# A two-layer perceiver: layer 0 stores each transposed memory in DRAM, layer 1 loads it and folds its layer norm into weights and one scale

## The chip, the core and the metric

The kernel runs on one core of one Trainium2 chip. The metric is the device time of one execution in microseconds. A core has TensorE (PE in the profile, with its weight loads listed apart as PEld), VectorE (DVE), ScalarE (ACT), GpSimd (POOL) and SyncE (SP, which here only issues DMAs). All data is float32.

## What is computed

The input is a query array x of 16 x 64 x 256 and a memory ctx of 16 x 1601 x 256. Six blocks are each added to x: cross attention over ctx with a top-32 softmax, retention and a transformer layer with a mixture of experts (layer 0); cross attention over ctx with 16 heads, random features and a tree of small networks (layer 1). Both cross attentions read the same memory. The one in layer 1 normalises it first:

```python
kn = layernorm(ctx, norm_w, norm_b)          # (ctx - mean) * rsqrt(var + 1e-5) * norm_w + norm_b
vn = layernorm(ctx, norm_w, norm_b)
K = (kn @ Wk + bk).reshape(b, s, H, E)       # s = 1601, H = 16, E = 16
V = (vn @ Wv + bv).reshape(b, s, H, E)
A = softmax(0.25 * einsum('blhe,bshe->bhls', Q, K))
out = einsum('bhls,bshd->blhd', A, V) + Q
```

## The kernel before

**Layer 0, cross attention** (lines 225 to 394) takes the 16 memories in 8 pairs. `turned_pair` (L237) loads the two memories of a pair with `load_mem` (L213: two DMAs on SP's queue, 1536 KB and 65 KB), rows on the partitions, and transposes them on TensorE (L248: 26 transposes for each memory) by way of PSUM; ScalarE copies the result into a tile `mT` of 128 x 2 x 1601 (L253), which holds the 256 features on partitions. The loop over chunks is outermost, so a 512-column chunk of one memory is complete after its second copy. `mT` has two buffers, one pair; the memories have six, three pairs. `scored_pair` (L284) multiplies queries by `mT` (L290), ScalarE scales the scores (L298), VectorE picks the top 32 of each row (`choose`, L302), and two iterations later `gather` (L325) reads the untransposed memory once more (L346). Only then is that memory's buffer free for a later pair's load.

**The middle** is retention (from L515) and the transformer layer (from L591). The work of layer 1 on memories 0, 1 and 2 that needs no query is written after it (L899 to L910), but the planner, which orders each engine's instructions by its own estimate of when they are ready, moves much of it up into the middle.

**Layer 1, cross attention** (L912 to L1169) works on one memory (batch) at a time, in 8 units each: 4 parts of the 1601 positions by 2 halves of the heads. For each unit u, the main loop (L1102) writes out this order for PE, VectorE and ScalarE: scores of u (`score`, L981); one step of the next batch's keys (`keys`, L460, L468); for four row groups a maximum on VectorE (L995) and an exponential on ScalarE (L997); transposes of unit u-1's exponentials (`turn_over`, L1010) with their copies (L1015, L1017); a step of the next batch's values (`values`, L482, L490); in units 1 to 3 a step of `collect` for the batch before (L1041), which uses VectorE, GpSimd (L1049, L1051, L1076 to L1085), ScalarE (L1050) and TensorE (L1062); from unit 3 on, four steps of the norm of memory b+3; one step of the turning of memory b+2; and the weighted sum of unit u-1 (`weigh`, L1029, L1036). GpSimd and SP are not under this written order: the planner sets theirs.

The norm (`normalise`, L408) and the turning (`turned_mem`, L432) are what the change touches. In batch b, memory b+3 is loaded a second time; VectorE takes its statistics (L415, L416), ScalarE a square root (L419), VectorE the reciprocal (L421), GpSimd subtracts the mean and scales the rows (L426, 13 instructions). One batch later TensorE transposes it (L439, 26 transposes in 8 steps) and ScalarE copies it into `mT`, applying norm_w and norm_b as scale and bias (L444, 8 copies). One batch after that, `keys` and `values` read `mT`. Here `memt` has two buffers, and `mT` two.

Of the kernel before, what the change touches and what calls it, by code (L numbers as in the profile page):

```python
# [9 lines left out]
F32 = mybir.dt.float32  # L10
# [6 lines left out]
P = 128  # L17
D = 256
# [11 lines left out]


KEY_STEPS = ((1, 0), (3, 0), (3, 1), (1, 1), (2, 0), (2, 1), (0, 0), (0, 1))
TURN_STEPS = ((3, 0), (3, 1), (1, 0), (1, 1), (2, 0), (2, 1), (0, 0), (0, 1))
VALUE_STEPS = (2, 1, 1, 2, 2, 2, 2, 1)
NEG = -3.0e38
MASKED = -1.0e30
# [29 lines left out]
def perceiver_kernel(  # L66
# [21 lines left out]
    nc = tc.nc  # L88
    const = ctx.enter_context(tc.tile_pool(name="const", bufs=1))
    small = ctx.enter_context(tc.tile_pool(name="small", bufs=3))  # L90

    def load_square(pool, src, n, name):
        t = pool.tile([P, n, 2, D], F32, name=name, tag=name)
# [131 lines left out]
    with ExitStack() as ph:  # L225
# [11 lines left out]
        def turned_pair(k, mems, memTs):  # L237

            for h in range(2):
                mems.append(load_mem(memp, 2 * k + h))  # L240
                memTs.append(work.tile([P, 2, S], F32, name="mT", tag="mT"))
            for n0, n in SCH:
                for h in range(2):
                    for dc in range(2):
                        pt = ps_m.tile([P, 512], F32, name="pt", tag="mm")
                        for j in range((n + P - 1) // P):
                            c = n0 // P + j
                            nc.tensor.transpose(  # L248
                                pt[:, j * P : j * P + chunk(c)],
                                mems[h][0 : chunk(c), c, dc * P : (dc + 1) * P],  # L250
                                ident[0 : chunk(c), 0 : chunk(c)],
                            )
                        nc.scalar.copy(memTs[h][:, dc, n0 : n0 + n], pt[:, 0:n])  # L253
                        yield

        first_mems, first_memTs = [], []
# [141 lines left out]

    x1 = ctx.enter_context(ExitStack())
    wp = x1.enter_context(tc.tile_pool(name="x1_w", bufs=1))  # L400
    memp = x1.enter_context(tc.tile_pool(name="x1_mem", bufs=2))
    kvp = x1.enter_context(tc.tile_pool(name="x1_kv", bufs=2))
    early = ExitStack()
    ps_early = early.enter_context(tc.tile_pool(name="x1_ps_e", bufs=2, space=PSUM))
    w_x = load_square(wp, w_x1, 4, "w_x")
    wq, wk, wv, wo = (w_x[:, i, :, :] for i in range(4))

    def normalise(mt):  # L408

        st = small.tile([P, NC, 6], F32, name="m_st", tag="m_st")  # L410
        mv = small.tile([P, NC, 2], F32, name="m_mv", tag="m_mv")
        nc.gpsimd.memset(mv[:, 12, :], 1.0)
        for c in range(NC):
            m = chunk(c)
            nc.vector.bn_stats(out=st[0:m, c, :], in_=mt[0:m, c, :])  # L415
            nc.vector.bn_aggr(out=mv[0:m, c, :], in_=st[0:m, c, :])  # L416
            yield
        sd = small.tile([P, NC], F32, name="m_sd", tag="m_sd")
        nc.scalar.activation(sd, mv[:, :, 1], AF.Sqrt, bias=eps)  # L419
        rstd = small.tile([P, NC], F32, name="m_rstd", tag="m_rstd")  # L420
        nc.vector.reciprocal(rstd, sd)  # L421
        nmean = small.tile([P, NC], F32, name="m_nmean", tag="m_nmean")
        nc.gpsimd.tensor_scalar(nmean, mv[:, :, 0], -1.0, None, ALU.mult)
        for c in range(NC):
            m = chunk(c)
            nc.gpsimd.tensor_scalar(  # L426
                mt[0:m, c, :], mt[0:m, c, :], nmean[0:m, c : c + 1], rstd[0:m, c : c + 1],
                ALU.add, ALU.mult,
            )
            yield  # L430

    def turned_mem(mt, mT, pool):  # L432

        for part, dc in TURN_STEPS:
            c0, nch, n = PARTS[part]
            pt = pool.tile([P, 512], F32, name="pt", tag="mm")
            for j in range(nch):
                c = c0 + j
                nc.tensor.transpose(  # L439
                    pt[:, j * P : j * P + chunk(c)],  # L440
                    mt[0 : chunk(c), c, dc * P : (dc + 1) * P],
                    ident[0 : chunk(c), 0 : chunk(c)],
                )
            nc.scalar.activation(  # L444
                mT[:, dc, c0 * P : c0 * P + n], pt[:, 0:n], AF.Identity,
                bias=col("L1_norm_b", dc), scale=col("L1_norm_w", dc),
            )
            yield

    def new_mT():  # L450
        return kvp.tile([P, 2, S], F32, name="mT", tag="mT")
# [1 line left out]
    def keys(mT, kT, pool):  # L453

        for part, oc in KEY_STEPS:
            c0, _, n = PARTS[part]
            n0 = c0 * P
            ps = pool.tile([P, 512], F32, name="ps_k", tag="mm")
            for dc in range(2):
                nc.tensor.matmul(  # L460
                    ps[:, 0:n],
                    lhsT=wk[:, dc, oc * P : (oc + 1) * P],
                    rhs=mT[:, dc, n0 : n0 + n],
                    start=(dc == 0),
                    stop=(dc == 1),
                )
            yield
            nc.scalar.activation(  # L468
                kT[:, oc, n0 : n0 + n], ps[:, 0:n], AF.Identity, bias=col("L1_bk", oc)
            )  # L470
            yield

# [26 lines left out]
            pool.tile([P, NC, D], F32, name="v", tag="v"),  # L499
        )  # L500

    mems, mTs, kvs, kvs_of = {}, {}, {}, {}

    def fetch(b):
        mems[b] = load_mem(memp, b)
        return normalise(mems[b])

    def run(steps):
        for _ in steps:
# [387 lines left out]


    for b in range(2):  # L899
        run(fetch(b))  # L900
    for b in range(2):
        mTs[b] = new_mT()
        run(turned_mem(mems.pop(b), mTs[b], ps_early))
        if b == 0:
            kvs[0] = new_kv(0)
            mT = mTs.pop(0)
            run(keys(mT, kvs[0][0], ps_early))
            run(values(mT, kvs[0][1], ps_early, nc.scalar.copy))
            run(fetch(2))
    early.close()  # L910

    with x1 as ph:  # L912
# [47 lines left out]
                )  # L960

        project_T(ps_m, wq, qnT, head_pairs)

        bqv = act.tile([P, D], F32, name="bqv")
        nc.gpsimd.tensor_tensor(bqv, row("L1_bq"), row("L1_bv"), ALU.add)
        qnat = act.tile([P, NB, D], F32, name="qnat", tag="b")
        project(
            ps_m, wq, qnT,
# [33 lines left out]
        def turn_over(part, a):  # L1002
# [92 lines left out]

        units = [(b, part, oc) for b in range(B) for part in range(NPART) for oc in range(2)]
        state = {}
        joining = made_k = made_v = turns = norms = iter(())
# [396 lines left out]
```

## Time and profile before

| what | value |
|---|---|
| time, median of 3 runs | 1710.52 us (1710.38 to 1710.7) |
| the profiled execution's own time | 1709.81 us |
| its span, first to last instruction | 1708.1 us |
| TensorE busy, matmuls | 1512.6 us (89% of the span) |
| VectorE, ScalarE, GpSimd busy | 1021.2, 814.6, 212.0 us |
| read from and written to HBM | 85.82 MB, 5.24 MB |
| layer 0's cross attention, to its last matmul | about 0 to 260 us |
| the middle | about 260 to 533 us |
| layer 1's cross attention, first scores to last weighted sum | 532.9 to 1408.0 us |

A row of the busy table is the union of an engine's instructions, so overlapping matmuls are counted once. The profile says of each group of instructions how many there are, how long they were busy together, the mean of one, and what ended the idle time before them. The chain of work follows the execution back from its last instruction, at each step to what released it; time on that chain is what an edit can win.

### The profile page before, as it was taken

The numbers are of one execution on the slowest core, as the hardware profiler recorded it, in microseconds if no ns is written. First come the engines' busy times: TensorE is split into PE (matmuls) and PEld (weight loads), VectorE is DVE, ScalarE is ACT, GpSimd is POOL, SyncE is SP. The second block draws the span as 40 slices with busy tenths as digits, with TensorE's granted clock in tenths as the row PEclk, the third lists the DMA queues.
The fourth block names the chain that finished last, engine by engine and source line by source line (L and its number), as shares of the span: only waits on it lengthen the run. The fifth ranks groups of instructions, "written<-read, shape, count | busy, mean of one in ns | idle before, by whom it ended". The sixth has DMA issues, their size and how long they took to land.

```text
span 1708.1 us, 27877 instructions
## 1 busy us (share of the span) xinstructions
PE 1512.6 (89%) x10992; PEld 1008.2 (59%) x10992; DVE 1021.2 (60%) x2197; ACT 814.6 (48%) x1984; POOL 212.0 (12%) x405
## 2 busy tenths in 40 slices
PE   4899979992939999999999999999999973889997
PEld 3555546672836666666666666666667652544455
DVE  2667847771145777677767776777766665333122
ACT  3455531350005766666667666766666551212121
POOL 0000004201010120222021202120210001000000
PEclk9999989995969999999999999999999996889999
DMA  9044203223910101110011101110100003100000
GB/s 316 1 154 138 94 19 108 83 91 97 287 58 1 40 3 41 40 41 15 29 40 41 34 11 41 40 41 3 41 2 3 3 3 122 66 1 0 0 0 25
DMA packets 76034, 92.84 MB, mean 54 GB/s; under 512 B 2408, under 2 KB 71072, under 8 KB 75776
## 3 DMA queue, kind: packets, MB, share of 16 engines
q1 hardware_dynamic: 72064, 80.85, 14.9%
q0 software_dynamic: 2688, 9.17, 1.9%
q8 instruction: 86, 1.41, 0.4%
q10 hardware_dynamic: 1152, 1.05, 0.2%
q14 instruction: 44, 0.36, 0.1%
HBM read 85.82 MB, written 5.24 MB: 53 GB/s over the span
## 4 chain that ended last, share of the span: by engine, by line
PE 72%; ACT 10%; DVE 9%; issue 4%; DMA 3%; SPq 1%; POOL 0%; ACTq 0%; DVEq 0%; POOLq 0%
PE ps_v L482 10%; PE ps_k L460 7%; ACT a L997 6%; PE sc L981 6%; PE po L1029 6%; PE pt L1010 5%; PE ps_h L1334 5%; PE ps_p L183 3%; PE ps_o L1352 3%; PE pt L248 3%; PE sc L290 3%; PE pu L346 3%; PE pt L439 2%; PE ps_n L197 2%; DVE nmax L995 2%
## 5 line engine op out<-in xcount | busy, mean ns | idle before, releaser
L997 ACT ACTIVATE a<-sc,nmax 128x384 f32<-128x384 f32 (+2 forms) x512 | 300.3, 596 | 170.8 <-DVE nmax L995 170.5
L995 DVE TENSOR_REDUCE nmax<-sc 128x1 f32<-128x384 f32 (+2 forms) x512 | 258.2, 567 | 109.8 <-PE sc L981 109.7
L482 PE MATMUL ps_v<-w_x,mT 128*128 128x256 f32 (+1 forms) x832 | 205.3, 385 | 22.3 <-ACT kT L468 22.3
L1010 PEld LDWEIGHTS pt<-ident,a 128*128 128x128 f32 (+1 forms) x1664 | 189.3, 141 | 52.1 <-issue 28.2
L1017 DVE COPY aT<-pt 128x512 f32<-128x512 f32 (+1 forms) x288 | 191.0, 685 | 37.8 <-PE pt L1010 30.8
L1010 PE MATMUL pt<-ident,a 128*128 128x128 f32 (+1 forms) x1664 | 207.5, 274 | 2.3 <-ACT kT L468 0.7
L460 PE MATMUL ps_k<-mT,w_x 128*128 128x384 f32 (+2 forms) x512 | 207.9, 528 | 0.1
L482 PEld LDWEIGHTS ps_v<-w_x,mT 128*128 128x128 f32 (+1 forms) x832 | 144.7, 186 | 49.6 <-ACT kT L468 31.3
L460 PEld LDWEIGHTS ps_k<-mT,w_x 128*128 128x128 f32 x512 | 87.4, 190 | 108.1 <-issue 77.6
L1029 PE MATMUL po<-aT,v 128*32 128x128 f32 (+1 forms) x3328 | 119.1, 277 | 10.9 <-DVE aT L1017 7.0
L444 ACT ACTIVATE mT<-pt,cols 128x384 f32<-128x384 f32 (+2 forms) x128 | 87.1, 684 | 79.0 <-PE pt L439 76.3
L981 PE MATMUL sc<-kT,qh 32*128 32x384 f32 (+2 forms) x1024 | 123.1, 548 | 0.0
L426 POOL TENSOR_SCALAR memt<-memt,m_nmean,m_rstd 128x256 f32<-128x256 f32 (+1 forms) x208 | 112.2, 557 | 7.3 <-PE po L1029 4.3
L997 ACT ACTIVATION_READ_ACCUMULATOR a<-sc,nmax 128x1 f32 x512 | 105.1, 205 | 0.0
L1029 PEld LDWEIGHTS po<-aT,v 128*32 128x32 f32 (+1 forms) x3328 | 82.7, 109 | 35.5 <-issue 13.5
L490 DVE COPY v<-ps_v 128x512 f32<-128x512 f32 (+1 forms) x120 | 69.2, 576 | 49.3 <-PE po L1029 30.7
L415 DVE BATCH_NORM_STATS2 m_st<-memt 128x6 f32<-128x256 f32 (+1 forms) x208 | 82.6, 401 | 3.4 <-DMA memt<-in_mem_dram 3.0
L1334 PE MATMUL ps_h<-xnT,fw 128*128 128x512 f32 x192 | 84.1, 596 | 0.0
L253 ACT COPY mT<-pt 128x512 f32<-128x512 f32 (+1 forms) x128 | 58.0, 503 | 53.3 <-PE pt L248 52.6
L248 PE MATMUL pt<-ident,memt 128*128 128x128 f32 (+1 forms) x416 | 63.2, 292 | 22.8 <-DMA memt<-in_mem_dram 21.6
L468 ACT ACTIVATE kT<-ps_k,cols 128x384 f32<-128x384 f32 (+2 forms) x128 | 76.0, 593 | 13.2 <-PE ps_k L460 13.2
L1015 ACT COPY aT<-pt 128x512 f32<-128x512 f32 x128 | 76.9, 601 | 0.7 <-PE pt L1010 0.7
(310 smaller groups left out, 1945.8 us busy)
## 6 DMA issues: line engine op xcount, KB each, us to landing
memt<-in_mem_dram SPq DMA_DIRECT2D x32, 1536.0 KB, 9.1
w<-in_moe_w_dram SPq DMA_DIRECT2D x16, 1024.0 KB, 5.1
fw<-in_fff_w_dram SPq DMA_DIRECT2D x6, 1024.0 KB, 12.8
memt<-in_mem_dram SPq DMA_DIRECT2D x32, 65.0 KB
w_x<-in_w_x_dram POOLq DMA_DIRECT2D x2, 1024.0 KB, 12.2
rows<-in_rows_dram POOLq DMA_DIRECT2D x1, 1430.5 KB, 9.9
X<-in_x_dram SPq DMA_DIRECT2D x1, 1024.0 KB
w_mha<-in_w_mha_dram POOLq DMA_DIRECT2D x1, 1024.0 KB
```

Source lines behind the costliest of these rows:

```text
L248: nc.tensor.transpose(pt[:, j * P : j * P + chunk(c)], mems[h][0 : chunk(c), c, dc * P : (dc + 1) * P], ident[0 : chunk(c), 0 : chunk(c)],)
L426: nc.gpsimd.tensor_scalar(mt[0:m, c, :], mt[0:m, c, :], nmean[0:m, c : c + 1], rstd[0:m, c : c + 1], ALU.add, ALU.mult,)
L444: nc.scalar.activation(mT[:, dc, c0 * P : c0 * P + n], pt[:, 0:n], AF.Identity, bias=col("L1_norm_b", dc), scale=col("L1_norm_w", dc),)
L460: nc.tensor.matmul(ps[:, 0:n], lhsT=wk[:, dc, oc * P : (oc + 1) * P], rhs=mT[:, dc, n0 : n0 + n], start=(dc == 0), stop=(dc == 1),)
L482: nc.tensor.matmul(ps[0 : chunk(c), j, :], lhsT=mT[:, dc, c * P : c * P + chunk(c)], rhs=wv[:, dc, :], start=(dc == 0), stop=(dc == 1),)
L981: nc.tensor.matmul(scs[j][:, 0:n], lhsT=qh[rs, oc, b, :, :], rhs=kT[rs, oc, c0 * P : c0 * P + n], start=True, stop=True,)
L995: nc.vector.reduce_max(out=nm, in_=sc[:, 0:n], axis=AX.X, negate=True)
L997: nc.scalar.activation(aj[:, 0:n], sc[:, 0:n], AF.Exp, bias=nm, accum_out=tot[:, blk, part : part + 1])
L1010: nc.tensor.transpose(pt[0:m, j * P : (j + 1) * P], a[j][:, c * P : c * P + m], ident)
L1017: nc.vector.tensor_copy(aT[0:m, :], pt[0:m, :])
L1029: nc.tensor.matmul(po[32 * j : 32 * j + 32, :], lhsT=v[0:m, c0 + c, blk * 32 : (blk + 1) * 32], rhs=aTs[c][0:m, j * P : (j + 1) * P], star ...
L1334: nc.tensor.matmul(ps, lhsT=fw1[:, f, dc, m * P : (m + 1) * P], rhs=xnT[:, dc, cs], start=(dc == 0), stop=(dc == 1),)
```

## The change

Layer 0, after the second copy of each chunk, writes that chunk of `mT` to a tensor `turned_d` in DRAM: 4 DMAs for each memory, 64 in all, on SP's queue. Layer 1 loads `turned_d[b]` into its `mT` with one DMA in place of transposing. The norm is split: norm_w goes into the rows of Wk and Wv, the mean over features is subtracted from those weights, so that the mean of a memory row drops out, and norm_b goes into the biases of keys and values; these happen once. What is left of the norm, the reciprocal deviation of each of the 1601 rows, now lies along the free axis of `mT`. It is found from the statistics as before, as exp(-0.5 ln(var + eps)) on ScalarE with one correcting step on GpSimd, written to DRAM, read back repeated over all partitions (`rb`, 128 x 1601), and multiplied into `mT` by GpSimd in 8 instructions (`scaled_mem`). The untransposed memory is still loaded in layer 1, for the statistics alone; it now has one buffer. One activation table is loaded ahead of the main loop.

```diff
+    kept = ctx.enter_context(tc.tile_pool(name="kept", bufs=1, space=bass.MemoryType.DRAM))
+    turned_d = [kept.tile([P, 2, S], F32, name=f"turned{b}", tag=f"turned{b}") for b in range(B)]
+    rstd_d = [kept.tile([NC * P], F32, name=f"rstd{b}", tag=f"rstd{b}") for b in range(B)]
...
                         nc.scalar.copy(memTs[h][:, dc, n0 : n0 + n], pt[:, 0:n])
+                        if dc == 1:
+                            nc.sync.dma_start(
+                                out=turned_d[2 * k + h][:, :, n0 : n0 + n],
+                                in_=memTs[h][:, :, n0 : n0 + n],
+                            )
                         yield
...
-    memp = x1.enter_context(tc.tile_pool(name="x1_mem", bufs=2))
+    memp = x1.enter_context(tc.tile_pool(name="x1_mem", bufs=1))
...
+    for c in range(2):
+        nc.gpsimd.tensor_scalar(nb[:, c, :], ones, col("L1_norm_b", c), None, ALU.mult)
...
+            nc.tensor.matmul(
+                ps[:, oc : oc + 1], lhsT=wk[:, c, oc * P : (oc + 1) * P],
+                rhs=col("L1_norm_b", c), start=(c == 0), stop=(c == 1),
+            )
+    nc.vector.tensor_tensor(kbias, ps, cols[:, at : at + 2], ALU.add)
+    nc.gpsimd.tensor_tensor(bqv, row("L1_bq"), row("L1_bv"), ALU.add)
...
+        nc.tensor.matmul(ps, lhsT=nb[:, c, :], rhs=wv[:, c, :], start=(c == 0), stop=(c == 1))
+    nc.vector.tensor_tensor(bqv, bqv, ps, ALU.add)
+    for wi in (wk, wv):
+        for c in range(2):
+            nc.gpsimd.tensor_scalar(wi[:, c, :], wi[:, c, :], col("L1_norm_w", c), None, ALU.mult)
...
+            nc.tensor.matmul(ps, lhsT=mean, rhs=wi[:, c, :], start=(c == 0), stop=(c == 1))
+        for c in range(2):
+            nc.vector.tensor_tensor(wi[:, c, :], wi[:, c, :], ps, ALU.subtract)
+    def deviations(b):
+        mt = load_mem(memp, b)
+        yield
...
             nc.vector.bn_stats(out=st[0:m, c, :], in_=mt[0:m, c, :])
             nc.vector.bn_aggr(out=mv[0:m, c, :], in_=st[0:m, c, :])
             yield
-        nc.scalar.activation(sd, mv[:, :, 1], AF.Sqrt, bias=eps)
-        nc.vector.reciprocal(rstd, sd)
-        nc.gpsimd.tensor_scalar(nmean, mv[:, :, 0], -1.0, None, ALU.mult)
-        for c in range(NC):
-            nc.gpsimd.tensor_scalar(
-                mt[0:m, c, :], mt[0:m, c, :], nmean[0:m, c : c + 1], rstd[0:m, c : c + 1],
-                ALU.add, ALU.mult,
-            )
-            yield
-    def turned_mem(mt, mT, pool):
...
+        nc.gpsimd.tensor_scalar(var, mv[:, :, 1], EPS, None, ALU.add)
+        nc.scalar.activation(rs, var, AF.Ln)
+        nc.scalar.activation(rs, rs, AF.Exp, scale=-0.5)
+        yield
+        nc.gpsimd.tensor_tensor(var, var, rs, ALU.mult)
+        nc.gpsimd.tensor_tensor(var, var, rs, ALU.mult)
+        nc.gpsimd.tensor_scalar(var, var, -0.5, 1.5, ALU.mult, ALU.add)
+        nc.gpsimd.tensor_tensor(rs, rs, var, ALU.mult)
+        nc.sync.dma_start(out=rstd_d[b].rearrange("(c p) -> p c", p=P), in_=rs)
+        rstds[b] = memp.tile([P, S], F32, name="rb", tag="rb")
+        nc.sync.dma_start(out=rstds[b], in_=rstd_d[b][0:S].partition_broadcast(P))
+        yield
+    def scaled_mem(b, mT):
+        nc.sync.dma_start(out=mT, in_=turned_d[b])
+        yield
+        rb = rstds.pop(b)
+        for c0, _, n in PARTS:
+            for dc in range(2):
+                sl = slice(c0 * P, c0 * P + n)
+                nc.gpsimd.tensor_tensor(mT[:, dc, sl], mT[:, dc, sl], rb[:, sl], ALU.mult)
+                yield
...
     for b in range(2):
-        run(fetch(b))
-    for b in range(2):
+        run(deviations(b))
         mTs[b] = new_mT()
-        run(turned_mem(mems.pop(b), mTs[b], ps_early))
+        run(scaled_mem(b, mTs[b]))
...
-            run(fetch(2))
+    run(deviations(2))
...
-                aT = work.tile([P, 512], F32, name="aT", tag="aT", bufs=5)
+                aT = work.tile([P, 512], F32, name="aT", tag="aT", bufs=6)
...
+            nc.scalar.preload_act_table_set("natural_log_exp_and_others")
...
-                        turns = turned_mem(mems.pop(b + 2), mTs[b + 2], ps_m)
+                        scaling = scaled_mem(b + 2, mTs[b + 2])
+                        next(scaling)
-                        norms = fetch(b + 3)
+                        norms = deviations(b + 3)
+                        next(norms)
...
-                if u % 8 == 7:
-                    run(norms)
-                next(turns, None)
+                next(scaling, None)
```

In the main loop the load of `mT` for b+2 and that of the memory b+3 are issued at the start of batch b, the statistics stay in units 3 to 6, the logarithm and the exponential fall in unit 6, and one multiplication by `rb` is written into each unit. `kbias` replaces `bk` in the copies of the keys (L468), and `bqv` moves up from L964.

More of the change, by code (lines that the diff above doesn't have):

```diff
@@ L32 @@
 KEY_STEPS = ((1, 0), (3, 0), (3, 1), (1, 1), (2, 0), (2, 1), (0, 0), (0, 1))
-TURN_STEPS = ((3, 0), (3, 1), (1, 0), (1, 1), (2, 0), (2, 1), (0, 0), (0, 1))
 VALUE_STEPS = (2, 1, 1, 2, 2, 2, 2, 1)
@@ L406, in perceiver_kernel @@
     wq, wk, wv, wo = (w_x[:, i, :, :] for i in range(4))
-    def normalise(mt):
+    mean = wp.tile([P, P], F32, name="mean")
+    nc.gpsimd.memset(mean, 1.0 / D)
+    nb = wp.tile([P, 2, P], F32, name="nb")
+    for c in range(2):
+        nc.gpsimd.tensor_scalar(nb[:, c, :], ones, col("L1_norm_b", c), None, ALU.mult)
+    kbias = wp.tile([P, 2], F32, name="kbias")
+    ps = ps_early.tile([P, 2], F32, name="ps_kb", tag="mm")
+    for oc in range(2):
+        for c in range(2):
[3 more added lines that the diff above has]
+            )
+    at = COLS["L1_bk"][0]
+    nc.vector.tensor_tensor(kbias, ps, cols[:, at : at + 2], ALU.add)
+    bqv = wp.tile([P, D], F32, name="bqv")
+    nc.gpsimd.tensor_tensor(bqv, row("L1_bq"), row("L1_bv"), ALU.add)
+    ps = ps_early.tile([P, D], F32, name="ps_vb", tag="mm")
+    for c in range(2):
+        nc.tensor.matmul(ps, lhsT=nb[:, c, :], rhs=wv[:, c, :], start=(c == 0), stop=(c == 1))
+    nc.vector.tensor_tensor(bqv, bqv, ps, ALU.add)
+    for wi in (wk, wv):
+        for c in range(2):
+            nc.gpsimd.tensor_scalar(wi[:, c, :], wi[:, c, :], col("L1_norm_w", c), None, ALU.mult)
+        ps = ps_early.tile([P, D], F32, name="ps_wm", tag="mm")
+        for c in range(2):
+            nc.tensor.matmul(ps, lhsT=mean, rhs=wi[:, c, :], start=(c == 0), stop=(c == 1))
+        for c in range(2):
+            nc.vector.tensor_tensor(wi[:, c, :], wi[:, c, :], ps, ALU.subtract)
+    rstds = {}
+    def deviations(b):
+        mt = load_mem(memp, b)
+        yield
         st = small.tile([P, NC, 6], F32, name="m_st", tag="m_st")
@@ L417, in normalise @@
             yield
-        sd = small.tile([P, NC], F32, name="m_sd", tag="m_sd")
-        nc.scalar.activation(sd, mv[:, :, 1], AF.Sqrt, bias=eps)
-        rstd = small.tile([P, NC], F32, name="m_rstd", tag="m_rstd")
-        nc.vector.reciprocal(rstd, sd)
-        nmean = small.tile([P, NC], F32, name="m_nmean", tag="m_nmean")
-        nc.gpsimd.tensor_scalar(nmean, mv[:, :, 0], -1.0, None, ALU.mult)
-        for c in range(NC):
-            m = chunk(c)
-            nc.gpsimd.tensor_scalar(
-                mt[0:m, c, :], mt[0:m, c, :], nmean[0:m, c : c + 1], rstd[0:m, c : c + 1],
-                ALU.add, ALU.mult,
-            )
-            yield
@@ L432, in turned_mem @@
-    def turned_mem(mt, mT, pool):
[L434 to L448, printed above, removed]
+        var = small.tile([P, NC], F32, name="m_var", tag="m_var")
@@ new lines, in deviations @@
+        nc.gpsimd.tensor_scalar(var, mv[:, :, 1], EPS, None, ALU.add)
+        rs = small.tile([P, NC], F32, name="m_rs", tag="m_rs")
+        nc.scalar.activation(rs, var, AF.Ln)
[6 more added lines that the diff above has]
+        nc.sync.dma_start(out=rstd_d[b].rearrange("(c p) -> p c", p=P), in_=rs)
@@ L468, in keys @@
             nc.scalar.activation(
-                kT[:, oc, n0 : n0 + n], ps[:, 0:n], AF.Identity, bias=col("L1_bk", oc)
+                kT[:, oc, n0 : n0 + n], ps[:, 0:n], AF.Identity, bias=kbias[:, oc : oc + 1]
             )
@@ L500, in new_kv @@
         )
[L502 to L506, printed above, removed]
+    mTs, kvs, kvs_of = {}, {}, {}
     def run(steps):
@@ L962, in perceiver_kernel @@
         project_T(ps_m, wq, qnT, head_pairs)
-        bqv = act.tile([P, D], F32, name="bqv")
-        nc.gpsimd.tensor_tensor(bqv, row("L1_bq"), row("L1_bv"), ALU.add)
         qnat = act.tile([P, NB, D], F32, name="qnat", tag="b")
@@ L1097, in perceiver_kernel @@
         state = {}
-        joining = made_k = made_v = turns = norms = iter(())
+        joining = made_k = made_v = scaling = norms = iter(())
         a = None
```

## The prediction, made before the result was known

> **What bounds the kernel now.** First the page, for the engine that sets the end.
>
> ```profile
> PE 1512.6 (89%) x10992; PEld 1008.2 (59%) x10992; DVE 1021.2 (60%) x2197; ACT 814.6 (48%) x1984; POOL 212.0 (12%) x405
> PE 72%; ACT 10%; DVE 9%; issue 4%; DMA 3%; SPq 1%; POOL 0%; ACTq 0%; DVEq 0%; POOLq 0%
> ```
>
> TensorE is 89% busy and carries 72% of the chain that ended last, so its work is worth removing; GpSimd and DMA carry 3% together. Then I cut the trace into stages: one pair of layer 0, and three batches of layer 1's main loop from one batch's first scores to the next's (starts read from the timeline: 1202.00, 1258.17, 1312.19, 1363.33). Columns: length, then busy time and count of each engine, granted clock, DMA share, GB/s.
>
> ```profile
> 133.40:156.78 23.38, 22.68 (x153) 12.67 (x151) 17.20 (x17) 12.63 (x25) 0.00 (x0) 1.00 0.45 141
> 1202.00:1258.17 56.17, 53.87 (x499) 37.88 (x495) 41.02 (x93) 37.60 (x101) 10.99 (x22) 1.00 0.11 32
> 1258.17:1312.19 54.02, 53.31 (x499) 37.83 (x495) 35.00 (x66) 35.12 (x98) 4.14 (x8) 1.00 0.02 3
> 1312.19:1363.33 51.14, 50.42 (x473) 34.70 (x469) 35.00 (x66) 29.79 (x90) 3.72 (x7) 1.00 0.02 3
> ```
>
> The last three rows are experiments that the loop's end makes for us. Batch 12 still norms and turns (as batches 0 to 12 do, each 56.17 us), batch 13 turns but has nothing left to norm, batch 14 does neither. All are bound by TensorE, also with the turning gone. In layer 0 TensorE is busy 22.68 of 23.38 us, while DMA is used to 0.45.
>
> The chain inside batch 12 shows one stretch where TensorE isn't what comes last.
>
> ```profile
> 1228.31 0.45 PE pt L1062 x4
> 1228.79 0.42 DVE parts L1068
> 1229.22 0.43 DVE parts L1068
> 1229.68 0.44 DVE m_st L415
> 1231.92 0.69 DVE v L490
> 1232.61 0.48 DVE nmax L995
> 1233.17 0.42 ACT a L997
> ...
> 1234.40 0.48 ACT kT L468
> 1234.93 1.99 PE ps_v L482 x8
> ```
>
> In unit 3 VectorE has a joining step, then four statistics, and comes late to the maxima of unit 4: that unit takes 8.17 us where batch 13's takes 6.51. The statistics stay after the change, and so does this.
>
> **What the Trainium skill says.** "ScalarE: Activation LUTs", What ACT_TABLE_LOAD costs and Table sets: a switch of table set costs 1283 ns plus a drain, and one set holds both exp and ln. The trace agrees on the load: 12 at L419 and 12 at L997 between 600 and 1420 us, each 1283 ns; the shared set isn't used yet. "SBUF — State Buffer", Who interferes with whom: VectorE with at most one SBUF input, outside its two-port modes, doesn't contend with GpSimd. It agrees: a copy aT at 1254.62, inside GpSimd's 7.01 us block at 1251.59, took 0.69 us, as one at 1225.75 outside it. "DMA: Bandwidth & Descriptors", Specifications: below 512 B a write is a read-modify-write; no row here shows 4 B writes, as the deviations' are. Same page, Queues, rings and completion order: an engine takes the descriptors of one ring in order, so SP's transfers queue behind each other; no row here tests it.
>
> **The main loop, removed.** Turning: batch 13 less batch 14, unit by unit, is 0.28 + 0.42 + 0.33 + 0.32 + 0.33 + 0.33 + 0.44 + 0.43 = 2.88 us. That is less than the 26 transposes' 4.1 us busy (L439, 0.27 us each with overlap), which is the difference between union and issue; I take the measured 2.88. The 8 copies on ScalarE (L444, 5.5 us) went with them in that comparison and are not counted again. Of the 2.88, unit 3's 0.32 is lost where the norm still runs: TensorE would only come sooner to scores whose maxima VectorE takes no sooner. Table loads: batch 12 less batch 13 is 2.15 us, of which unit 4 is 1.66 (statistics, stays) and unit 7 is 6.76 - 6.07 = 0.69. Unit 7 is where the return to exp (1.28 us, then exponentials, then a key copy) makes ps_v wait 0.42 us; one set for all removes it. I credit 0.69. So 2.88 - 0.32 + 0.69 = 3.25 us for each of 13 batches and 2.88 for batch 13: **45.1 us**.
>
> **The main loop, added.** (1) GpSimd's product. Priced from its own two-input rows: 128x256 takes 0.727 us (L1076) and 128x2048 takes 5.311 (L734), so 2.56 ns an element and 0.07 us each; 8 instructions over 3202 elements are 8.2 + 0.6 = 8.8 us, against 13 x 0.557 = 7.2 removed. GpSimd is idle 45 us of a batch, and nobody needs `mT` until the next one, so: nothing by itself. But its place moves, into units 1 and 2, beside `collect`. The load of 1.64 MB is issued at the batch's start; the same-sized memory load takes 9.1 us, so products run from about +9 to +18 us. `collect`'s first step wants GpSimd at 1214.52, +12.5 us; ScalarE's L1050 waits for it (0.3 us now) with its later exponentials queued behind. If it waits out one product in progress, at most 1.3 us, it mostly fits the 0.7 us before the next copy and 1.2 us before the next exponential. I take 0.15 us x 14 = **2 us**, from 0 to the case of rival B. (2) Ln, Exp: two ScalarE instructions of some 0.25 us in unit 6, where two loads of 1.28 us and the root's 0.31 leave; a GpSimd hop of about 0.5 us before them, at 1249.8, falls into ScalarE's 1.28 us of former table load. Nothing; half a microsecond for each batch at most. (3) Deviations out in 1664 words, back as 0.82 MB: for 1024 rows of 64 B the trace has 2.7 us (by_head). I allow 3 to 10 us and about 4 us back. Behind them on SP stand the next `mT` and memory loads; statistics start +20 us into the batch, and 10 + 4 + two loads at some 5 us each and latency still arrive by about +15. Nothing. (4) Bytes: 4.1 MB in 53 us is 77 GB/s of the 350 seen. Nothing.
>
> **Layer 0.** 64 writes, 3.28 MB a pair. The stage moves 141 GB/s at a share of 0.45; doubled it is 282 at 0.9, which fits, barely. What counts is the moment.
>
> ```profile
> 114.87 0.37 SPq L215 DMA_DIRECT2D memt<-in_mem_dram  x1
> 116.18 0.37 SPq L215 DMA_DIRECT2D memt<-in_mem_dram  x1
> ```
> ```profile
> 123.03 0.66 PE L248 MATMUL pt<-ident,memt 128*128 128x128 f32 x4
> 128.45 0.66 PE L248 MATMUL pt<-ident,memt 128*128 128x128 f32 x4
> ```
> ```profile
> GB/s 0 0 0 0 0 0 0 0 0 12 195 142 285 386 379 357 348 358 357 299 350 343 353 346 346 345 253 12 0 0 0 0 0 27 0 0 0 0 0 0
> ```
>
> SP issues a pair's two loads as soon as buffers are free; TensorE turns the first from 123.03 and the second from 128.45. In the last fence (110 to 134 us in 40 slices) the loads run at 350 GB/s from about 116 to 126.5. The first lands near 122, so about 0.8 us of slack. By the copies' times one chunk's write (0.52 MB, 1.7 us at the stage's 316 GB/s) is likely to stand in front: late by 1.7 - 0.8 = 0.9 us, for each of five such loads (pairs 3 to 7): **5 us**, between 0 (SP orders loads first) and rival A. Waiting for `mT`'s writes before its next use costs nothing: a chunk's buffer is refilled 23 us later.
>
> **The middle.** 52 transposes leave, but those of memory 0 (295 to 300.8) fill TensorE's wait for VectorE's layer norm, and those of memory 1 (372.8 to 379) its wait for y1: gain near 0. Added are some 14 small matmuls for weights and biases, about 3 us, after the weights land (L405 issued 260.74). Keys 0 now wait for load, statistics, deviations out and back, and 8.8 us of products, so their 4.3 us at 300 to 306 move to later; from 391 to 418 TensorE is empty. I take **3 us**, between -6 and +12.
>
> **Sum.** -45 + 2 + 5 + 3 = -35. The profiled execution, 1709.81 (span 1708.1 and 1.7 around it), stands 0.7 under the median: 1674.8 + 0.7 gives **1675**.
>
> **Rivals.** *A, slower: loads behind writes.* If the planner puts all of a pair's writes ahead of the next loads on SP, those wait for the pair's last copy (about 121.5 where the issue is at 114.87: 6.6 us) and for three undrained writes (1.1 MB, 3.5 us): late by 6.6 + 3.5 - 0.8 = 9.3 us, five times 46; 1710.5 - 45 + 46 + 5 = **1717**. It decides from 8 us of lateness. For it: the code writes before it loads. Against: the planner goes by readiness, and has issued loads early. *B, also slower in full: GpSimd late for `collect`.* If all 8 products stand ahead of L1049, ScalarE waits until +18, 5.5 us, of which 1.9 is spare: 3.6 x 14 = 50 less the 2; 1675 + 48 = **1723**, and half of it 1699. *C, more gain.* TensorE wins the whole 4.1 us of transposes and unit 4's 1.66 as well: 4.1 + 0.69 + 1.66 = 6.5 x 13 + 4 = 88, middle and layer 0 free: **1622**; against it, batch 14 still takes 51.14 without either. That the turned memory isn't used can't be: `turned_mem` is gone.
>
> **Chances.** Forecast's own case, 1655 to 1692: 0.68. C, in part (1622 to 1655): 0.10. B in part, 1692 to 1707: 0.09; same, 0.04. A or B in full: 0.09. Range 1650 to 1702: it leaves about 0.06 below and 0.14 above. Runs tell apart 0.2% (3.4 us). Faster 0.87, same 0.04, slower 0.09.
>
> **What would show it.** Batches of 52.5 to 53.5 us; unit 4 still about 8 us; no table load inside the loop; layer 0 pairs of about 24.3 us, with transposes waiting for memt; GpSimd products done by +20 us. I am wrong if a batch is over 55 us, if pairs pass 27 us, or if L1050 waits over 2 us.

## The result, and the profile after

The changed kernel takes 1871.9 us (median of 4 runs, 1868.09 to 1876.47) against 1710.61 us (1710.38 to 1711.22): a ratio of 1.0943, 95% interval 1.0919 to 1.0968. It is 161 us slower where 35 us less were forecast. The profiled execution took 1871.47 us (span 1869.7).

First the page of the kernel after: the busy time of the engines, and the chain that ended last.

```profile
PE 1510.7 (81%) x10596; PEld 995.7 (53%) x10596; DVE 1021.5 (55%) x2187; ACT 737.3 (39%) x1879; POOL 244.4 (13%) x396
PE 57%; DMA 16%; DVE 9%; POOL 7%; ACT 7%; issue 3%; SPq 1%; ACTq 0%; POOLq 0%; DVEq 0%
```

TensorE has 396 instructions less, as it should (416 transposes gone, 20 small matmuls added), but it carries only 57% of the chain; GpSimd and DMA carry 23% together, where they had 3%.

Then the same stretches as before: a pair of layer 0 (first row) and batches 12, 13 and 14 of the main loop (length, then busy time and count of PE, PEld, DVE, ACT, POOL, granted clock, DMA share, GB/s). The first row comes from its own query of the kernel after.

```profile
125.03:150.10 25.07, 22.55 (x152) 14.07 (x152) 17.29 (x17) 12.33 (x25) 0.00 (x0) 0.93 0.87 265
```
```profile
1346.64:1412.06 65.42, 53.38 (x472) 36.51 (x469) 40.93 (x92) 32.16 (x93) 12.68 (x20) 0.92 0.13 41
1412.06:1474.73 62.67, 53.18 (x473) 36.66 (x469) 34.94 (x66) 29.37 (x89) 11.58 (x15) 0.92 0.12 42
1474.73:1525.87 51.14, 50.43 (x473) 34.70 (x469) 34.99 (x66) 29.70 (x89) 3.70 (x7) 1.00 0.01 2
```

Batch 14, which turned nothing before and scales nothing now, still takes 51.14 us. Batches 1 to 13 take 62.7 to 65.5 us, with TensorE busy 53 of them; batch 0, which scales too but has no earlier batch to collect, takes 47.8 us. By unit (starts of the scores), batch 7 takes 6.57, 6.69, **18.28**, 6.61, 8.17, 6.18, 6.50 and 5.63 us. With 6.5 in unit 2 the sum would be 52.9 us, which is the forecast's 56.17 - 3.25. So the gain came, and one unit takes back more than three times as much. Over the 13 batches that stall, unit 2 exceeds 6.5 us by 152 us in all.

The chain of one stall, batch 7 (it starts at 1023.92), read from four timelines: SP's queue, GpSimd, ScalarE, TensorE.

```profile
1016.92 0.38 SPq L219 DMA_DIRECT2D memt<-in_mem_dram  x1
1021.01 0.37 SPq L475 DMA_DIRECT2D rstd<-m_rs  x1
...
1031.90 0.33 SPq L477 DMA_DIRECT2D rb<-rstd  x1
1032.28 0.43 SPq L482 DMA_DIRECT2D mT<-turned  x1
```
```profile
1041.12 7.91 POOL L488 TENSOR_TENSOR mT<-mT,rb 128x512 f32<-128x512 f32 x8 [20.13 <-DMA mT<-turned]
1048.98 0.24 POOL L1082 TENSOR_TENSOR wt<-low,nmax 128x32 f32<-128x32 f32 x1
```
```profile
1035.52 0.60 ACT L1048 COPY aT<-pt 128x512 f32<-128x512 f32 x1
1049.25 0.23 ACT L1083 ACTIVATE wt<-wt 128x32 f32<-128x32 f32 x1 [13.13 <-POOL wt L1082]
1049.39 0.25 ACT L1069 COPY pos<-po 128x128 f32<-128x128 f32 x1
```
```profile
1049.69 1.11 PE L1043 MATMUL pt<-ident,a 128*128 128x128 f32 x4 [9.43 <-ACT pos L1069]
```

SP sends the deviations out at 1021.01 and waits 10.9 us for them to land before it can ask for them back; the load of the turned memory stands behind that. GpSimd, in its own order, has all eight products ahead of `collect`'s small difference `wt` (0.24 us), and waits for both loads. VectorE has had the operand of `wt` ready since 1036.02. ScalarE wants `wt` from 1036.1 on, and waits 13.13 us with the copy `pos` and unit 2's exponentials behind it; TensorE then waits for ScalarE. In batch 12 of the kernel before, GpSimd took the same step as soon as VectorE was done, and ScalarE waited 0.26 us for it:

```profile
1214.52 0.24 POOL L1049 TENSOR_TENSOR wt<-low,nmax 128x32 f32<-128x32 f32 x1 [12.09 <-DVE low L1047]
1214.79 0.23 ACT L1050 ACTIVATE wt<-wt 128x32 f32<-128x32 f32 x1 [0.26 <-POOL wt L1049]
```

**Layer 0** costs 7.1 us (the projection after it starts at 253.6 instead of 246.5). **The middle** costs 50.0 us more: from there to layer 1's query projection it takes 319.9 us instead of 269.9. These are the two largest new ones among TensorE's waits in the kernel after (total us, times, longest):

```profile
PE ps_kb L428 <- DMA w_x<-in_w_x_dram: 11.4, 1, 11.4
PE ps_p L187 <- DMA w_mha<-in_w_mha_dram: 8.4, 1, 8.4
```

The first is the preparation of the weights, which the planner put ahead of the retention in TensorE's order. It waits for `w_x` and then takes 6.9 us itself. The second shows in GpSimd's timeline: the load of `w_mha`, issued at 295.78 before the change (first fence), now stands behind memory 0's products and behind memory 1's variance and correcting steps (second fence).

```profile
295.78 0.96 POOL L94 DMA_DIRECT2D w_mha<-in_w_mha_dram  x1 [1.05 <-issue]
```
```profile
321.46 7.93 POOL L488 TENSOR_TENSOR mT<-mT,rb 128x512 f32<-128x512 f32 x8 [15.91 <-DMA rb<-rstd]
329.48 0.25 POOL L466 TENSOR_SCALAR m_var<-m_mv 128x13 f32<-128x13 f32 x1
...
332.95 0.98 POOL L98 DMA_DIRECT2D w_mha<-in_w_mha_dram  x1 [0.27 <-issue]
```

### The profile page after: what moved, and what is told of

It reads as the page before. It is cut to its first block, busy times and chain, and to the rows that moved or that the text cites. A ratio compares the mean times of both kernels' runs of the same rounds, so it can differ in the third digit from the quotient of the medians.

```text
span 1869.7 us, 27127 instructions
## 1 busy us (share of the span) xinstructions
PE 1510.7 (81%) x10596; PEld 995.7 (53%) x10596; DVE 1021.5 (55%) x2187; ACT 737.3 (39%) x1879; POOL 244.4 (13%) x396
## 4 chain that ended last, share of the span: by engine, by line
PE 57%; DMA 16%; DVE 9%; POOL 7%; ACT 7%; issue 3%; SPq 1%; ACTq 0%; POOLq 0%; DVEq 0%
PE ps_v L523 9%; PE ps_k L501 7%; POOL mT L488 6%; PE pt L1043 5%; DMA mT<-turned 5%; PE ps_h L1368 4%; PE sc L1014 4%; PE po L1062 4%; DMA rstd<-m_rs 4%; PE ps_o L1386 3%; ACT a L1030 3%; DMA memt<-in_mem_dram 3%; PE ps_p L187 2%; PE pt L252 2%; PE pu L355 2%
## 5 line engine op out<-in xcount | busy, mean ns | idle before, releaser
L1043 PE MATMUL pt<-ident,a 128*128 128x128 f32 (+1 forms) x1664 | 225.8, 284 | 125.5 <-ACT pos L1069 117.2
L1043 PEld LDWEIGHTS pt<-ident,a 128*128 128x128 f32 (+1 forms) x1664 | 196.3, 146 | 185.1 <-ACT pos L1069 120.3
L523 PE MATMUL ps_v<-w_x,mT 128*128 128x256 f32 (+1 forms) x832 | 214.5, 398 | 19.3 <-ACT kT L509 19.3
L523 PEld LDWEIGHTS ps_v<-w_x,mT 128*128 128x128 f32 (+1 forms) x832 | 152.4, 195 | 43.8 <-ACT kT L509 24.4
L488 POOL TENSOR_TENSOR mT<-mT,rb 128x384 f32<-128x384 f32 (+2 forms) x128 | 127.4, 1032 | 337.8 <-DMA mT<-turned 268.1
L1069 ACT COPY pos<-po 128x128 f32<-128x128 f32 x128 | 33.6, 262 | 152.8 <-PE po L1062 152.7
L509 ACT ACTIVATE kT<-ps_k,kbias 128x384 f32<-128x384 f32 (+2 forms) x128 | 76.1, 595 | 5.7 <-PE ps_k L501 4.7
```

Source lines behind the costliest of these rows:

```text
L488: nc.gpsimd.tensor_tensor(mT[:, dc, sl], mT[:, dc, sl], rb[:, sl], ALU.mult)
L523: nc.tensor.matmul(ps[0 : chunk(c), j, :], lhsT=mT[:, dc, c * P : c * P + chunk(c)], rhs=wv[:, dc, :], start=(dc == 0), stop=(dc == 1),)
L1043: nc.tensor.transpose(pt[0:m, j * P : (j + 1) * P], a[j][:, c * P : c * P + m], ident)
```

## The experiments

The first theory was: in the loop GpSimd's order makes the stall (T1) and SP's order its size (T2); in the middle the prepared weights cost 18 us (T3), and small work behind GpSimd's products the rest (T4); layer 0's writes cost 7 by themselves (T5). The rival to all of it was that the added transfers or products slow the stages simply by being there (R).

e2 to e7 and e9 were each executed once. The kernels that were executed several times spread over 4 to 10 us, and the start of the projection after layer 0, a stage that e2 to e9 leave as it is, lies anywhere from 248.4 to 254.9 us in them. So where two kernels differ by a few us, the stage in the trace is the evidence, and not the total time.

**The writes alone**, on the kernel before:

```diff
...
                         nc.scalar.copy(memTs[h][:, dc, n0 : n0 + n], pt[:, 0:n])
+                        if dc == 1:
+                            nc.sync.dma_start(
+                                out=turned_d[2 * k + h][:, :, n0 : n0 + n],
+                                in_=memTs[h][:, :, n0 : n0 + n],
+                            )
```

> The kernel before with the 64 writes of the turned memories added and nothing else; nobody loads them back. Theory (layer 0's loads are late behind writes, about a microsecond for each pair, and that is all the writes cost): the first matmul of the projection after layer 0 starts at about 253.7 us, where it started at 246.66 before and at 253.77 after, and the time is 1717 to 1718 us. Rival (the writes cost nothing, and the 7 us come from layer 1's memory loads being asked for early): 1710 to 1712. Rival (the writes also keep later transfers busy and so carry part of the loss of the middle): 1725 or more.

Measured: 1716.7 us (1712.25 to 1718.92), ratio 1.0043 (1.0026 to 1.006). In the profiled run, the lowest of the four, the projection starts at 250.1. The writes cost 4 to 7 us and nothing later: the middle takes 269.2 us, as before. The stretch from 140 to 190 us, in the kernel before (first row) and in this one:

```profile
140.00:190.00 50.00, 48.60 (x327) 27.63 (x325) 36.83 (x35) 27.23 (x55) 0.00 (x0) 1.00 0.49 155
140.00:190.00 50.00, 44.22 (x310) 26.82 (x309) 34.27 (x33) 24.94 (x51) 0.00 (x0) 1.00 0.90 269
```

**`collect`'s small operations on VectorE**, the rest of the changed kernel as it is:

```diff
-            nc.gpsimd.tensor_tensor(wt, low.unsqueeze(2).to_broadcast(wide), nmax, ALU.subtract)
+            nc.vector.tensor_tensor(wt, low.unsqueeze(2).to_broadcast(wide), nmax, ALU.subtract)
             nc.scalar.activation(wt, wt, AF.Exp)
-            nc.gpsimd.tensor_tensor(tot, tot, wt, ALU.mult)
...
             yield
+            nc.vector.tensor_tensor(tot, tot, wt, ALU.mult)
```

> The changed kernel, with the two small operations of collect (the difference of the maxima, and the product with tot) on VectorE instead of GpSimd, the second one a unit later. Theory T1 (GpSimd's order, which has collect's difference behind all 8 products, is what stops the loop): unit 2 of a batch falls from 18.3 to 6.5 to 7 us, a batch from 64.6 to about 53, ScalarE's exponential of collect waits under 1 us instead of 13, and the time falls by 14 times 11.7 to about 1707 us. Rival R (the added transfers or the long products themselves slow the loop): unit 2 stays above 15 us and the time at about 1870. Between them: the products, still late, then hold something else, such as the keys of the next memory: 1720 to 1780.

Measured: 1719.4 us, 152 less than the changed kernel's profiled run. Unit 2 takes 6.50 us. Unit 3 takes 6.6 to 7.4: two steps of `collect` on VectorE that read two tiles from SBUF (L1086, L1090) take 0.18 and 0.19 us where no product runs on GpSimd, and up to 1.30 and 1.12 us beside one. Eight units in a row, from the last of batch 11 on:

```profile
1210.39:1263.29 52.90, 50.83 (x473) 34.77 (x469) 41.61 (x95) 32.37 (x93) 12.29 (x18) 1.00 0.25 80
```

T1 holds: every transfer and every product is still there, in batches of 52.9 to 53.7 us. R falls for the loop, but for the part of a microsecond in unit 3. The expectation of 1707 had counted 14 stalls; there are 13, since nothing is collected in batch 0.

**The deviations on another queue**:

```diff
-        nc.sync.dma_start(out=rstd_d[b].rearrange("(c p) -> p c", p=P), in_=rs)
+        nc.gpsimd.dma_start(out=rstd_d[b].rearrange("(c p) -> p c", p=P), in_=rs)
...
-        nc.sync.dma_start(out=rstds[b], in_=rstd_d[b][0:S].partition_broadcast(P))
+        nc.gpsimd.dma_start(out=rstds[b], in_=rstd_d[b][0:S].partition_broadcast(P))
```

> The changed kernel, with the write of the deviations and their load back issued from GpSimd's queue instead of SP's, so that the load of the turned memory no longer stands behind them. Theory T2 (the size of the stall comes from SP's order: the load of the turned memory waits for the deviations to land): that load is issued at the batch's start, products begin about 8 us earlier, unit 2 falls from 18.3 to about 10.5 us, and the time to about 1763 (1740 to 1790). Rival (the products are late for another reason, the load's own length or the buffer that comes free late): unit 2 stays at 17 to 19 us and the time at 1860 to 1880.

Measured: 1885.5 us, unit 2 still 18 to 22 us. T2 falls. SP now issues the turned memory at the start of batch 10, at 1223.37, but GpSimd's timeline of this kernel shows that the products wait as long:

```profile
1221.38 1.23 POOL L475 DMA_DIRECT2D rstd<-m_rs  x1 [0.29 <-POOL m_rs L474]
1232.37 0.58 POOL L477 DMA_DIRECT2D rb<-rstd  x1 [9.75 <-DMA rstd<-m_rs]
1241.65 7.90 POOL L488 TENSOR_TENSOR mT<-mT,rb 128x512 f32<-128x512 f32 x8 [8.70 <-DMA rb<-rstd]
```

What is late is the deviations themselves: out and back takes 20 us, whichever queue carries it. That became T2b, which `e7` tests below.

**The weights prepared later.** The block from `mean` to the subtraction of `ps_wm` is moved down, as it is, to stand before these lines:

```diff
+    mean = x1_wp.tile([P, P], F32, name="mean")
...
     for b in range(2):
         run(deviations(b))
```

> The changed kernel, with the preparation of layer 1's weights (biases and mean) moved down in the program to just before the deviations of memories 0 and 1, so that its matmuls stand behind the retention in TensorE's order. Theory T3 (these matmuls, which wait for w_x in front of the retention, cost about 18 us): the idle stretch of 11.4 us before the first of them goes, and the time falls to about 1854 us. Rival (the waits of the middle follow one another, and the next one, for the weights w_mha or for keys 0, takes the place): 1866 to 1872.

Measured: 1856.0 us. T3 holds: from the projection after layer 0 to layer 1's query projection the middle takes 301.4 us instead of 319.9 (269.9 before the change).

**Five pieces of work taken off GpSimd**, on top of that:

```diff
-        nc.gpsimd.tensor_scalar(var, mv[:, :, 1], EPS, None, ALU.add)
+        near = nc.vector if b < 3 else nc.gpsimd
+        near.tensor_scalar(var, mv[:, :, 1], EPS, None, ALU.add)
...
-        w = load_square(wp, w_mha, 4, "w_mha")
+        w = load_square(wp, w_mha, 4, "w_mha", nc.sync)
...
-        nc.gpsimd.dma_start(out=wg, in_=w_gate.rearrange("(c p) e -> p c e", p=P))
+        nc.sync.dma_start(out=wg, in_=w_gate.rearrange("(c p) e -> p c e", p=P))
...
-        nc.gpsimd.tensor_tensor(
+        nc.vector.tensor_tensor(
             X, X, row("ln2_b").unsqueeze(1).to_broadcast([P, NB, D]), ALU.add
...
-            nc.gpsimd.tensor_scalar(wi[:, c, :], wi[:, c, :], col("L1_norm_w", c), None, ALU.mult)
+            nc.vector.tensor_scalar(wi[:, c, :], wi[:, c, :], col("L1_norm_w", c), None, ALU.mult)
```

> The changed kernel with the weights prepared late, as in e4, and besides: for memories 0 to 2 the variance step ahead of Ln on VectorE, the loads of w_mha and wg on SP's queue, X += ln2_b on VectorE, the scaling of the weights on VectorE. Theory T4 (what e4 leaves of the middle's loss is work standing behind products on GpSimd: the load of w_mha, the variance in front of Ln, the weights' scaling): the projections of the attention in the middle start at about 313 us instead of 332, 6 us behind the kernel before as layer 0 is, and the time is about 1837 us (1833 to 1842). Rival (the deviations' round trip through DRAM, 11 us out and 5 back, is what is late, and nothing on GpSimd): 1850 to 1857.

Measured: 1854.1 us, the projections at 329.3: a miss, inside the rival's range. The time hides a part of the gain: the middle takes 295.4 us, 6.0 less than in e4, but the stalls of the loop, which vary from run to run, take 3 more. SP's timeline of this kernel says why the projections are late.

```profile
313.29 0.36 SPq L446 DMA_DIRECT2D rstd<-m_rs  x1
313.82 0.63 SPq L98 DMA_DIRECT2D w_mha<-in_w_mha_dram  x1
```

The load of `w_mha` has only changed queues: on SP it stands behind the write of memory 1's deviations, whose last step waits on GpSimd for the same products. TensorE waits 13.0 us for it. The rival isn't refuted: those products start at 303.9, when memory 0's deviations have come back, 16 us after they went out.

**GpSimd under the written order**, on the changed kernel alone, with the products written after `collect`'s steps:

```diff
-        order = {mybir.EngineType.PE, mybir.EngineType.DVE, mybir.EngineType.Activation}
+        order = {mybir.EngineType.PE, mybir.EngineType.DVE, mybir.EngineType.Activation,
+                 mybir.EngineType.Pool}
...
-                next(scaling, None)
+                if u % 8 >= 3:
+                    for _ in range(2):
+                        next(scaling, None)
```

> The changed kernel with GpSimd put under the loop's written order, as the three other engines are, and the products written two in a unit from unit 3 on, behind collect's two small operations. Theory T1 (it is only GpSimd's order): unit 2 at 6.5 us with collect's operations still on GpSimd, batches of 52.9 us, the time as with those on VectorE, 1715 to 1722. Rival (VectorE's doing these operations sooner was what helped, or products that end later now hold the next memory's keys): a batch of 55 us or more, 1745 and up.

Measured: 1715.6 us, unit 2 at 6.50, batches of 52.9. In GpSimd's timeline of this kernel `wt` now goes first, the moment VectorE is ready, and the products follow 19 us later:

```profile
1119.90 0.24 POOL L1082 TENSOR_TENSOR wt<-low,nmax 128x32 f32<-128x32 f32 x1 [13.41 <-DVE low L1080]
...
1138.98 6.32 POOL L488 TENSOR_TENSOR mT<-mT,rb 128x512 f32<-128x512 f32 x6
```

T1 is shown twice, by two edits that share no line.

**Earlier statistics**, GpSimd's order left bad:

```diff
-                if u % 8 >= 3:
-                    for _ in range(4):
+                if u % 8 >= 2:
+                    for _ in range(6):
                         next(norms, None)
```

> The changed kernel with the statistics taken six in a unit from unit 2 on, where they were taken four in a unit from unit 3: the deviations go out about 14 us sooner, GpSimd's order stays. Since moving the deviations to another queue changed nothing, the new theory T2b: the size of the stall is the round trip of the deviations (write some 10.5 us, load back some 9, from the end of unit 6 on), and only then the load of the turned memory. Then products start when that load lands, some 9 us into the batch, and unit 2 takes 9 to 11 us: 1750 to 1785 us. Rival (the turned memory's own load sets it too, by its buffer or its order on SP): unit 2 still over 15 us, 1840 to 1875.

Measured: 1781.5 us, inside what T2b expected, but by luck: unit 2 was to take 9 to 11 us. In this kernel the products start when the turned memory lands, 6 us into the batch (batch 10, start 1158.05), and all eight are over when `wt` is wanted: ScalarE waits 2.0 us for it, and unit 2 takes 6.50 (6.5 to 7.4 over the batches).

```profile
1164.10 7.99 POOL L488 TENSOR_TENSOR mT<-mT,rb 128x512 f32<-128x512 f32 x8 [22.78 <-DMA mT<-turned]
1172.05 0.24 POOL L1082 TENSOR_TENSOR wt<-low,nmax 128x32 f32<-128x32 f32 x1
```

The batch still takes 58.0 us, because of the cure: six statistics in a unit bring VectorE late to the maxima, in units 3 and 4 (VectorE is the third of the busy times).

```profile
1171.38:1177.88 6.50, 6.42 (x72) 4.66 (x68) 5.18 (x13) 3.64 (x12) 1.16 (x3) 1.00 0.00 0
1177.88:1187.06 9.18, 7.10 (x64) 4.88 (x60) 7.21 (x21) 3.57 (x11) 0.00 (x0) 1.00 0.01 2
1187.06:1197.78 10.72, 8.16 (x61) 5.46 (x57) 8.19 (x23) 6.19 (x14) 3.49 (x6) 0.84 0.21 50
```

So the stall needs both: the products ahead of `wt`, and the deviations late.

**Both repairs together**, the edits of e5 and e6:

> The changes of e5 and e6 together. If the two causes are independent and are all, the time is that of e6 less what e5 gains, 1719 - 34 = 1685 us (1678 to 1690), 1.5% under the kernel before, and what is left against the forecast of 1675 is layer 0 and the rest of the middle. Rival (the stage in the middle and the loop's start share a cause, so that gains overlap): 1695 or more.

Measured: 1693.1 us (1689.48 to 1696.6), ratio 0.9892 (0.9872 to 0.9912): 1.1% faster than before the change. It lies between the expectation, which had been set before e5 missed, and the rival, and decides for neither. From e6 it is 22.5 us less.

**The load of `w_mha` on ScalarE's queue**, on e8:

```diff
-        w = load_square(wp, w_mha, 4, "w_mha", nc.sync)
+        w = load_square(wp, w_mha, 4, "w_mha", nc.scalar)
```

> The kernel of e8 with the load of w_mha issued from ScalarE's queue. There the load had only changed queues: on SP it stood behind the write of the deviations of memory 1, which waits for GpSimd's products of memory 0, and TensorE waited 13.0 us for it. Theory T4b (the middle waits for w_mha, and that waits for the products through whichever in-order queue it is put in): issued from ScalarE right after the second Exp, at about 305 us instead of 317, it lets the projections of the attention start at 320 to 323 us instead of 332.5, and the time falls from 1693 to about 1682 (1678 to 1686). Rival (the load is late because its transfer shares the DMA with others, whatever the issue): 1689 or more.

Measured: 1682.3 us. The load is issued at 308.02, and the projections start at 319.85, when TensorE waits 0.5 us for its other operand. The wait for `w_mha` is gone, and T4 holds for this load, once it is out of every queue that waits for GpSimd's products. The rival may have a part: the load is issued 8.9 us sooner than in e8, but the projections start 12.6 us sooner, as it also lands faster (within 11.8 us of its issue, where e8 took 15.5). What makes it land faster isn't shown.

**Layer 0's writes on GpSimd's queue**, on the kernel of e1:

```diff
-                            nc.sync.dma_start(
+                            nc.gpsimd.dma_start(
                                 out=turned_d[2 * k + h][:, :, n0 : n0 + n],
```

> The kernel before with layer 0's 64 writes alone, issued from GpSimd's queue instead of SP's. Theory T5 (what layer 0 loses is the order on SP: loads behind writes): the loads come as before, the projection after layer 0 starts at 246.5 to 248 us, and the time is 1710 to 1712.5, 4 to 6 us under the same writes on SP (1716.7). Rival (the bytes cost it: read and write at once use the DMA to 0.9, whatever the queue): 1715 to 1719.

Measured: 1741.7 us (1740.65 to 1744.42), ratio 1.0189 (1.0172 to 1.0206). Both expectations missed; taking the writes out of SP's order costs another 25 us. Loads and writes now run at once, and both land later: a memory in 14.2 us (10.8 with the writes on SP), a 512 KB chunk in 8.1 (5.2). ScalarE's waits for `mT`'s buffer in this kernel (5.7 us in e1) show one consequence:

```profile
ACT mT L255 <- DMA turned<-mT: 17.4, 5, 4.4
```

So T5, that SP's order is what layer 0 loses, isn't borne out: the writes cost less in that order than beside it. Why isn't shown: the edit changes the order, but also the kind of queue (`software_dynamic` in the profile for GpSimd's, `hardware_dynamic` for SP's), and no run parts the two. Nor is it shown that these waits are the whole of the 25 us.

**All of it**: e9 with the writes on GpSimd's queue, and one thing more. In e9 memory 2's products still stood among the dispatch's transfers on GpSimd, and TensorE waited 31.8 us for the dispatched tokens (28.7 before).

```diff
-                if u % 8 >= 3:
-                    for _ in range(2):
+                if u % 8 >= (3 if u >= 8 else 6):
+                    for _ in range(2 if u >= 8 else 4):
                         next(scaling, None)
```

> The kernel of e9, with layer 0's writes on GpSimd's queue and the products of memory 2, which stood among the dispatch's transfers on GpSimd, written behind the statistics of the first batch. If each of the three costs named is what it seems, 1682 - 5 (layer 0) - 4 (the dispatch) = about 1673 us (1668 to 1679), near the forecast of 1675, whose sum then stands but for the orders of the queues. Rival (layer 0's cost is the bytes; the wait after the dispatch is the experts' weights): 1680 to 1684.

Measured: 1699.3 us (1697.33 to 1707.78), ratio 0.9943 (0.9928 to 0.9958). Both expectations missed. The wait for the dispatch is 28.7 us again; the writes take away more, as in e10.

**The same with the writes on SP**:

> The kernel of e9 with the products of memory 2, which stood among the dispatch's transfers on GpSimd, written behind the statistics of the first batch; layer 0's writes are on SP again. Theory: the wait for the dispatched tokens falls from 31.8 to 28.7 us, as before the change, and the time from 1682 to about 1679 us (1676 to 1682), a ratio of 0.9815 to the kernel before, 4 us over the forecast of 1675. Rival (the products of memory 2 now delay the keys of batch 1): 1682 or more.

Measured: **1678.8 us** (1677.85 to 1683.65), ratio 0.9828 (0.9814 to 0.9841) to the kernel before, and 193 us under the changed kernel. The time is the expected one, but hardly for the reason given. The wait for the dispatched tokens is 28.7 us again, yet the middle is only 0.4 us shorter than in e9 (279.5 against 279.9), as TensorE reaches that wait later; the rest of the 3.5 us lies in layer 0 and behind the loop, which this edit doesn't touch, and is no more than e12's own runs spread. One batch of it, and its chain:

```profile
1178.30:1231.16 52.86, 50.78 (x473) 34.73 (x469) 40.83 (x92) 32.38 (x93) 12.92 (x21) 1.00 0.18 51
```
```profile
PE 68%; DVE 11%; ACT 9%; DMA 8%; issue 3%; SPq 1%; POOL 0%; ACTq 0%; DVEq 0%; POOLq 0%
```

GpSimd has left the chain; DMA has 8% of it, where it had 3% before the change. Where the stages stand (start of each projection in the profiled runs, us; e8's profiled run is its slowest, 1696.6):

| kernel | after layer 0 | middle's attention | layer 1's queries | time |
|---|---|---|---|---|
| before | 246.5 | 306.0 | 516.4 | 1710.6 |
| changed | 253.6 | 349.3 | 573.5 | 1871.9 |
| e4, weights late | 252.9 | 332.1 | 554.3 | 1856.0 |
| e8, with e6's order | 254.9 | 332.5 | 547.9 | 1693.1 |
| e9, `w_mha` on ScalarE | 254.0 | 319.8 | 533.9 | 1682.3 |
| e12 | 252.7 | 318.9 | 532.2 | 1678.8 |

## Why the prediction was wrong

**The main loop, removed: right.** 3.25 us a batch were credited. Repaired batches take 52.86 us, 3.31 less than 56.17, and unit 4 keeps its 8.17 us. (Batch 0 took 51.22 us before, not the 56.17 given to batches 0 to 12; its gain is 3.3 to 3.5 us all the same.) One reason behind it was wrong: the two table loads did not leave. In the loop after there is one ahead of each Ln and one ahead of each Exp, 12 and 12 between 640 and 1430 us. The 0.69 us came all the same: unit 7 takes 5.63 us instead of 6.76, 1.13 less, of which 0.43 is the turning. The trace shows the return to exp in unit 6 now, right behind Ln (1018.29), and no longer ahead of unit 7's exponentials: this term came out right by luck. The forecast's sign "no table load inside the loop" was wrong.

**The main loop, added (1): the step that failed.** It let the products run "from about +9 to +18 us" and `collect` wait out "one product in progress, at most 1.3 us", 2 us in all. They run from +17.2 to +25.1 us (1041.12 and 1049.03 against 1023.92), and `wt` waits out all eight: 152 us. Two faults lie in it. The first is that +9 lets the turned memory's load start with the batch. Step (3) of the same sum had that load stand on SP behind the deviations, whose values the products need too. It let the two loads behind them arrive "by about +15", and called that nothing because it compared it with the statistics and not with the products. Its pieces were near: 10.9 us out against 3 to 10 allowed, some 9 back (e3) against 4, and 7.9 us of products against 8.8. Put together with all eight products, +15 and 8.8 less the 12.5 at which `wt` is wanted and 1.9 spare gives 9.4 us a batch, 122 us in 13: four fifths of what happened. The second is that GpSimd's place for the products was taken from the order of the program, which doesn't bind GpSimd; the planner put all eight ahead of `wt`. Rival B named that mechanism with 50 us, again from +18; its mechanism was right, and its size a third of what came. In full it shared a chance of 0.09 with rival A.

**The middle: 3 us were taken, 50 came.** "Gain near 0" was reasoned from what leaves; the failure is in what was added. The small matmuls (some 14 in the forecast, 20 in the trace) were given 3 us "after the weights land", and nothing for what stands behind them: they wait 11.4 us for `w_x` and take 6.9, with the retention behind them (e4: 18.5 us of the middle). "Keys 0 ... move to later" did not ask who else is in GpSimd's queue behind those products: the load of `w_mha` (e9: 13.1 us) and the variance steps and others of e5 (6.0 us together, not singly). e6's order took another 2.4 (e5 to e8). Some 10 us are left in e12: the middle takes 279.5 us there against 269.9. They were not taken apart.

**Layer 0: right in size, partly in reason.** 5 us forecast, 4 to 7 measured in e1 and the changed kernel (2 to 8 in the runs that leave layer 0 as changed), with pairs of 25.1 us (24.3 expected). TensorE waits 30.6 us for `memt` in e1 instead of 21.6. The DMA share is 0.87 to 0.90, as worked out. That the order on SP is the reason isn't shown: another queue, of another kind, made it worse. That waiting for `mT`'s writes "costs nothing" was not quite so: ScalarE waits 5.7 us for them in e1.

**The sum.** In e12 layer 0 costs 6.2 us and the middle 9.6; the part from layer 1's queries to batch 15 gains 45.9 where 45.1 less 2 was forecast, and the rest 1.0. That is -31 where -35 was forecast: the arithmetic of the loop's gain stands, in a kernel whose orders are repaired, and the middle is 6.6 us dearer than forecast even there. What was missing was the order in which engines not under the written order would do the added work, and the time at which its operands land.

## What to carry to other kernels

When a small operation of an in-order engine is on somebody's path, ask of every operation put on that engine when its *last* operand lands, and assume that all of them stand ahead of the small one unless an order is written down. Work a DMA round trip through DRAM into the time of its consumer, not of its issuer. Moving a late load to another queue helps only if that queue doesn't itself wait for the same work (e5 against e9).

## What the runs showed that was not expected

A write of 1664 single words (6.5 KB) takes 9.4 to 11.3 us to land from SP in the loop of the changed kernel, behind a memory load, and 10.4 to 14.9 us from GpSimd's queue in e3, without one ahead of it in that queue: the ring's order isn't what makes it slow. Nor is it a load beside it: in the changed kernel the last write (1409.22 to 1419.34) has none, with a DMA share of 0.07 meanwhile, and takes 10.1 us. What in the write takes the time isn't shown. The Trainium skill, "DMA: Bandwidth & Descriptors", Issuing engines are not separate DMA queues, says that DMAs of all issuing engines share the same 16 DMA engines and interleave; e10 agrees, with loads landing in 14.2 instead of 10.8 us. The same skill's "ScalarE: Activation LUTs", Table sets, gives one load for ln followed by exp. Here that doesn't hold, although the program asks for the shared set ahead of the loop: each Ln and each Exp of the deviations has its own load of 1283 ns.
